# A three-layer graph network on one core: comparisons of the first layer written for two groups of edges at a time

## The chip, the cores and the metric

The kernel runs on one core of one Trainium2 chip. The metric is device time in microseconds (us) for one execution of the whole program. Before the change the median of three runs is 2081.6 us (2081.57 to 2082.88). Profiles come from one further execution with the hardware profiler on; times inside a profile count from its first instruction.

## The reference, cut to what matters

There are 6250 nodes with 256 features and 100000 edges sorted by their target. Each of three graph layers multiplies by a weight matrix and sums the rows of the neighbours, scaled by the degrees of both ends.

```python
src = concatenate([edge_index[0], loops])        # every node is also its own neighbour
dst = concatenate([edge_index[1], loops])
deg = segment_sum(ones, dst); dinv = rsqrt(deg)
norm_edge = dinv[src] * dinv[dst]
for W, b in ((W1, b1), (W2, b2), (W3, b3)):      # 256 -> 512 -> 512 -> 256
    h = relu(segment_sum((h @ W)[src] * norm_edge[:, None], dst) + b)
return layernorm(x + h)
```

## The kernel before, in words

The nodes are cut into 50 blocks of 125 (`Q`). A layer needs, for each block, the sum over all edges that end in it. There are two ways to get this sum.

**Gathered blocks.** For blocks 22 to 49 of layer 1 (`every[FEW:]`), GpSimd (POOL) issues indirect DMAs that fetch 128 source rows at a time (L1192). The VectorE (DVE) compares target numbers with the columns 0 to 124 to make a 0/1 matrix `shot` (L1143), and TensorE (PE) multiplies the two into a sum (L1219). One fetch is one *chunk* of the schedule; layer 1 has 451 chunks. Product and fetch stand 5 chunks apart, later 8 (`SPLIT`).

**Dense blocks.** For blocks 0 to 21 (`few`) the kernel builds the 125 x 6250 matrix of edge counts and multiplies it by all of x: 50 products of 125x125 by 125x512 per block (L1283), 1100 in all. The counts come as bytes; ScalarE (ACT) casts five 125-column cuts at a time into a `piece` (L1151).

**Making the counts** is the generator `counts`, which also serves seven more blocks for later layers: 29 blocks in all. Each block has 25 groups of at most 128 edges (`GB`), one group for 5 target nodes. For a group, DVE makes two 0/1 matrices by comparison (`compared`, L799): `hot_lo`, 125 columns, for the source's place in its block, and `hot_key`, 250 columns, for the source's block and the target's place among 5. One bf16 product of the two (L866) gives 125 x 250 counts in PSUM. Two groups share a PSUM bank, and ACT writes both as bytes into a *place* (L828). When all 25 are there, DVE adds the self loops (L819), the counts are stored to HBM (`kept`), and the dense products of that block may begin from the next chunk on (`there`). The comparisons are written for five groups together (`WIDE`): 625 elements of `hot_lo`, then 750 and 500 of `hot_key`. Their operands are `near_cols`, fp32 numbers in PSUM, and `slots`, bf16 numbers in SBUF, and they write bf16.

**The order of the work** is written out by hand: `layer` walks over the chunks, and in each it emits a fetch, the product of an earlier fetch, one step of each waiting generator (`go`, `go_fixed`) and up to three dense products. Each engine then works through its own list in that order. `counts` yields twice in five of its steps, so 25 groups take 10 chunks. A product for the counts is emitted four steps behind its comparison. Banks come from the list `common`; at most three counted banks may wait for ACT (`COUNTING`). Dense products are due from chunk `first` = 16 on, at 50 per 19 chunks, never more than three in a chunk.

Around the start of layer 1, `parts` (x split in a high and a low part, one slice per block) is ready for blocks 20 to 49; `other_parts` (L1485, L1487) makes blocks 15-19, then 0-4, 5-9 and 10-14 in the first chunks. The places for the counts lie on the memory from which these are made. `both_stored` stores `parts` to HBM meanwhile, and `windows` looks up the next groups of edges. At the end of layer 1, `teams` (L993 and what feeds it) begins to load its data over the upper blocks of `parts` when all but 16 dense products are emitted.

`after1` finishes a block: L1304 transposes, L1330 multiplies by the weights, L1335 and L1338 add the bias and scale.

## Time and profile before

| | us |
|---|---|
| median of three runs | 2081.6 |
| the profiled execution | 2088.76 |
| its span, first to last instruction | 2086.9 |
| PE busy in the span | 1937.8 |
| DVE busy in the span | 1350.6 |
| comparisons for the counts (L799), 75 to 700 us | 324.87 |

The profiled execution is 7.2 us above the median, of which 1.9 us lie outside its span. The mean granted TensorE clock is 0.981. Layer 1 lies at about 75 to 700 us of the span, layer 2 follows until about 1650 us, and layer 3 ends it. In the lists below, "PE" is a matmul and "PEld" the load of its stationary operand; a count such as x2 is how many instructions were merged in a row, and what stands in brackets is the idle time of the engine before the row and what ended it. A matmul's end is modelled: one that takes 270 ns in a row can be followed by the next after about 110 ns.

### The profile page before, as it was taken

The numbers are of one execution on the slowest core, as the hardware profiler recorded it, in microseconds if no ns is written. First come the engines' busy times: TensorE is split into PE (matmuls) and PEld (weight loads), VectorE is DVE, ScalarE is ACT, GpSimd is POOL, SyncE is SP. The second block draws the span as 40 slices with busy tenths as digits, with TensorE's granted clock in tenths as the row PEclk, the third lists the DMA queues.
The fourth block names the chain that finished last, engine by engine and source line by source line (L and its number), as shares of the span: only waits on it lengthen the run. The fifth ranks groups of instructions, "written<-read, shape, count | busy, mean of one in ns | idle before, by whom it ended". The sixth has DMA issues, their size and how long they took to land.

```text
span 2086.9 us, 28961 instructions
## 1 busy us (share of the span) xinstructions
PE 1937.8 (93%) x8642; PEld 1516.1 (73%) x8642; DVE 1350.6 (65%) x2385; ACT 1266.8 (61%) x2230; POOL 1406.4 (67%) x1442
## 2 busy tenths in 40 slices
PE   4499999999999788989999999999988899999997
PEld 3377777777776566778888778886766677877785
DVE  6877888887882376777677777766666234434444
ACT  2566777787784566666666666666554455555552
POOL 2467777766777377777776776676666277777775
PEclk9999999999999899999999999999999999999998
DMA  8898999999999999999999999988897599999998
GB/s 173 248 300 218 275 259 255 273 255 261 272 274 254 266 259 257 256 253 273 262 259 262 261 261 264 264 240 239 243 278 232 150 282 291 294 291 298 293 291 219
DMA packets 266157, 540.24 MB, mean 259 GB/s; under 512 B 44142, under 2 KB 77857, under 8 KB 265990
## 3 DMA queue, kind: packets, MB, share of 16 engines
q0 software_dynamic: 157728, 360.04, 63.2%
q1 hardware_dynamic: 94980, 168.96, 29.8%
q10 hardware_dynamic: 13282, 9.30, 1.7%
q8 instruction: 70, 1.15, 0.2%
q14 instruction: 97, 0.79, 0.1%
HBM read 464.28 MB, written 73.87 MB: 258 GB/s over the span
## 4 chain that ended last, share of the span: by engine, by line
PE 63%; DMA 15%; issue 7%; POOL 5%; ACT 3%; DVE 3%; SPq 0%; POOLq 0%; ACTq 0%; DVEq 0%
PE sacc L1219 12%; DMA room<-tab,ssrc 8%; PE smm L1283 7%; PE win_ps L1283 7%; PE mat_ps L1283 7%; PE sacc L1283 5%; DMA back<-tab,ssrc 4%; PE win_ps L1385 4%; POOL room L1192 4%; PE win_ps L1401 2%; PE sacc L1330 2%; PE str L1283 2%; PE sacc L993 1%; PE sacc L866 1%; PE mat_ps L993 1%
## 5 line engine op out<-in xcount | busy, mean ns | idle before, releaser
L1192 POOL DMA_INDIRECT room<-tab,ssrc x442 | 465.2, 1053 | 192.5 <-issue 81.7
L1219 PE MATMUL sacc<-halves,shot 128*125 128x512 f32 x1541 | 535.3, 409 | 25.2 <-ACT halves L1250 11.2
L1151 ACT CAST piece<-room 125x625 fp32r<-125x625 uint8 x501 | 358.0, 723 | 211.5 <-PE win_ps L1283 72.5
L1192 POOL DMA_INDIRECT halves<-both,ssrc x384 | 361.3, 941 | 142.0 <-issue 40.4
L1192 POOL DMA_INDIRECT halves<-tab,ssrc x336 | 317.2, 944 | 103.6 <-PE sacc L1219 26.5
L1219 PEld LDWEIGHTS sacc<-halves,shot 128*125 128x125 f32 x1541 | 288.3, 188 | 114.5 <-DVE halves L1253 21.6
L799 DVE TENSOR_TENSOR back<-near_cols,slots 128x625 bf16<-128x625 f32 (+2 forms) x435 | 324.9, 801 | 29.7 <-PE sacc L866 12.8
L1143 DVE TENSOR_TENSOR shot<-near_cols,sdlo 128x500 fp32r<-128x500 f32 x371 | 247.4, 668 | 134.3 <-PE sacc L1219 128.5
L1253 DVE TENSOR_TENSOR halves<-room,halves 128x512 fp32r<-128x512 f32 x334 | 227.0, 691 | 121.2 <-ACT halves L1250 114.9
L1192 POOL DMA_INDIRECT back<-tab,ssrc x230 | 231.7, 1008 | 109.1 <-issue 38.6
L1250 ACT CAST halves<-room 128x512 fp32r<-128x512 f32 x334 | 202.1, 618 | 154.2 <-DMA room<-tab,ssrc 125.4
L1385 PE MATMUL win_ps<-back,w_sb 128*128 128x250 f32 x768 | 185.3, 385 | 13.8 <-ACT back L1362 10.8
L1283 PE MATMUL smm<-parts,piece 125*125 125x512 f32 x655 | 188.7, 405 | 1.6 <-ACT piece L1151 1.6
L1283 PE MATMUL win_ps<-parts,piece 125*125 125x512 f32 x650 | 185.2, 404 | 0.0
L1385 PEld LDWEIGHTS win_ps<-back,w_sb 128*128 128x128 f32 x768 | 148.6, 195 | 39.4 <-ACT back L1362 12.9
L1283 PE MATMUL mat_ps<-parts,piece 125*125 125x512 f32 x600 | 172.0, 404 | 0.5 <-ACT piece L1151 0.5
L866 PEld LDWEIGHTS <-back 128*125 128x125 bf16 x725 | 96.0, 138 | 73.5 <-issue 22.9
L1283 PE MATMUL sacc<-parts,piece 125*125 125x512 f32 x450 | 147.7, 432 | 0.9 <-ACT piece L1151 0.9
L828 ACT CAST room<-sacc 125x500 uint8<-125x500 f32 (+1 forms) x155 | 107.5, 711 | 55.5 <-PE sacc L866 41.0
L1283 PEld LDWEIGHTS win_ps<-parts,piece 125*125 125x125 f32 x650 | 119.4, 188 | 30.0 <-issue 2.5
L1283 PEld LDWEIGHTS smm<-parts,piece 125*125 125x125 f32 x655 | 116.8, 187 | 29.4 <-issue 2.3
L1253 DVE TENSOR_TENSOR halves<-back,halves 128x512 fp32r<-128x512 f32 x136 | 93.1, 691 | 65.4 <-ACT halves L1250 64.5
(337 smaller groups left out, 3304.8 us busy)
## 6 DMA issues: line engine op xcount, KB each, us to landing
parts<-tab SPq DMA_DIRECT2D x76, 448.0 KB
kept<-room SPq DMA_DIRECT2D x29, 683.6 KB
room<-kept SPq DMA_DIRECT2D x29, 683.6 KB
both<-parts SPq DMA_DIRECT2D x10, 1120.0 KB
tab<-st SPq DMA_DIRECT2D x50, 224.0 KB
own_row<-tab SPq DMA_DIRECT2D x38, 224.0 KB
parts<-kept SPq DMA_DIRECT2D x60, 136.7 KB
room<-tab,ssrc POOLq DMA_INDIRECT x442, 6.2
```

Of the source, the lines that this page charges most:

```text
L799: nc.vector.tensor_tensor(out, near_cols[:, :shape[2]].unsqueeze(1).to_broadcast(shape), numbers.unsqueeze(2).to_broadcast(shape), op=ALU. ...
L828: nc.scalar.copy(place[:, :, u * G:(u + len(ms)) * G].rearrange("p k (t r) -> p t k r", r=G), counted_in[:Q, :len(ms) * 256].rearrange("p ...
L866: nc.tensor.matmul(bank[:Q, len(pair) * 256:][:, :G * NB], lhsT=hot_lo, rhs=hot_key, start=True, stop=True)
L993: nc.tensor.matmul(team_banks[n][:, :TEAM * Q], lhsT=both_parts[u % 3][:, h * HID + n * P:h * HID + (n + 1) * P], rhs=team_pieces[(g * CUT ...
L1143: nc.vector.tensor_tensor(hot[:, :n], near_cols[:, :Q].unsqueeze(1).to_broadcast([P, n, Q]), dlo.rearrange("p b j -> p (b j)")[:, at:at + ...
L1151: nc.scalar.copy(piece, made_or_read[:, c * PIECE:(c + 1) * PIECE, :])
L1192: nc.gpsimd.indirect_dma_start(out=row, out_offset=None, in_=table, in_offset=bass.IndirectOffsetOnAxis(ap=at, axis=0))
L1219: nc.tensor.matmul(acc[:Q, :size], lhsT=hot, rhs=row[:, c0:c0 + size], start=(i == 1 and k == c0 == 0), stop=(k == KF and c0 + size == row ...
L1250: nc.scalar.copy(halves[:, :width], landed[chunk - hi_lag])
L1253: nc.vector.tensor_sub(halves[:, width:], landed.pop(chunk - lo_lag), halves[:, :width].bitcast(F32))
L1283: nc.tensor.matmul(acc_d[:Q], lhsT=got[done // PIECE][:, k % PIECE, :], rhs=parts[:, k], start=(k == 0), stop=(k == NB - 1))
L1385: nc.tensor.matmul(h_ps[:, f, :], lhsT=w2_sb[:, k, (f2 + f) * P:(f2 + f + 1) * P], rhs=zt[:, k, :], start=(k == 0), stop=(k == KH - 1))
```

## The change

It does three things, in layer 1 alone.

1. **Comparisons.** Groups go in units of two, 12 units and one single group per block. `slots` gets a pitch of 26 for 25 groups, so that each pair begins on a 4-byte boundary. The column numbers for the comparison stand in PSUM as bf16, each number twice in a row (`near_keys`). The outputs are laid out with the two groups of a unit next to each other in each column, so that numbers, columns and output all have two 16-bit elements in their innermost dimension. `hot_lo` is compared for two units at once, 500 elements; `hot_key` per unit, 500 elements; the last group alone with 125 and 250 elements. The operands of L866 are then read with a step of two elements.
2. **Steps.** The first block's counts are emitted with three yields of their own in place of ten, later blocks with ten in 13 steps; products follow their comparison by two steps. `first` becomes 12.
3. **Order of the dense products.** Each dense block starts with row blocks 20 to 49, then takes 15-19, 10-14, 5-9 and 0-4. `other_parts` makes 0-4 first, then 5-9, 15-19, 10-14. `teams` starts to load when all but 15 products are emitted.

```diff
+TAIL = 4
-WIDE = 5
+TWO = 2
+WIDE = 2 * TWO
...
-    slots = one.enter_context(tc.tile_pool(name="sslots", bufs=1, side="right")).tile([P, NW, 2, Q], BF16, name="slots")
+    numbered = one.enter_context(tc.tile_pool(name="sslots", bufs=1, side="right"))
+    slots = numbered.tile([P, NW, 2, Q // GB, GB + 1], BF16, name="slots")
+    keys = numbered.tile([P, G * NB, 2], BF16, name="keys")
...
-            nc.vector.tensor_copy(keys, keys_i)
+            nc.vector.tensor_copy(keys, keys_i.unsqueeze(2).to_broadcast([P, G * NB, 2]))
...
-    near_cols = near[:, :G * NB]
-    nc.vector.tensor_copy(near_cols, keys)
+    near_cols = near[:, :Q]
+    nc.vector.tensor_copy(near_cols, cols[:, :Q])
+    nc.vector.tensor_copy(near[:, P:P + G * NB], keys.rearrange("p k t -> p (k t)").bitcast(F32))
+    near_keys = near[:, P:P + G * NB].bitcast(BF16).rearrange("p (k t) -> p k t", t=2)
...
         def compared(out, numbers):
-            shape = list(out.shape)
-            nc.vector.tensor_tensor(out, near_cols[:, :shape[2]].unsqueeze(1).to_broadcast(shape),
-                                    numbers.unsqueeze(2).to_broadcast(shape), op=ALU.is_equal)
+            _, pairs, wide, size = out.shape
+            nc.vector.tensor_tensor(out, near_keys[:, :wide, :size].unsqueeze(1).to_broadcast([P, pairs, wide, size]),
+                                    numbers.rearrange("p (j t) -> p j t", t=size).unsqueeze(2).to_broadcast([P, pairs, wide, size]),
+                                    op=ALU.is_equal)
...
-        total = len(blocks) * GB
+        units = [(n, u, min(TWO, GB - u)) for n in range(len(blocks)) for u in range(0, GB, TWO)]
+        total = len(units)
...
-            if s < total and s % WIDE == 0:
-                t, w = divmod(blocks[s // GB] * GB + s % GB, Q)
-                hot_stores.rotate(-1)
...
-                compared(hot_lo, slots[:, t, 0, w:w + WIDE])
-                compared(hot_key[:, :3], slots[:, t, 1, w:w + 3])
-            if s < total and s % WIDE == 2:
...
-                compared(hot[s // WIDE][1][:, 3:], slots[:, t, 1, w:w + WIDE - 3])
+                t, row = divmod(blocks[n], Q // GB)
+                at = u // TWO % 2 if size == TWO else 0
+                if size < TWO:
+                    alone = hot_stores[-1][:, WIDE * (Q + G * NB):].rearrange("p (j v t) -> p j v t", j=1, t=1)
+                    hot_lo, hot_key = alone[:, :, :Q], alone[:, :, Q:]
+                elif at == 0:
+                    hot_stores.rotate(-1)
...
+                if at == 0:
+                    width = min(WIDE, GB - u)
+                    compared(hot_lo, slots[:, t, 0, row, u:u + width])
+                compared(hot_key[:, at:at + 1, :, :size], slots[:, t, 1, row, u:u + size])
+                hot[s] = [(hot_lo[:, at, :, v], hot_key[:, at, :, v]) for v in range(size)]
             copied(ticks)
-            m = s - 4
+            m = s - TWO
...
-                nc.tensor.matmul(bank[:Q, len(pair) * 256:][:, :G * NB], lhsT=hot_lo, rhs=hot_key, start=True, stop=True)
...
-            if s % WIDE in (2, 4):
+                for v, (hot_lo_v, hot_key_v) in enumerate(hot.pop(m)):
+                    nc.tensor.matmul(bank[:Q, v * 256:][:, :G * NB], lhsT=hot_lo_v, rhs=hot_key_v, start=True, stop=True)
+                full.append((ticks + COPIED, bank, [n * GB + u + v for v in range(size)]))
+            if s % (GB // TWO + 1) % 4 != 3 and (s > GB // TWO or s % 2):
                 ticks += 1
                 yield 1
...
-        while products < FEW * NB - KF:
+        while products < FEW * NB - HOME // PIECE * PIECE:
...
+            c = order[c]
             nc.scalar.copy(piece, made_or_read[:, c * PIECE:(c + 1) * PIECE, :])
...
+        order = (*range(TAIL, CUTS), *range(TAIL - 1, -1, -1)) if i == 0 else range(CUTS)
...
-                    nc.tensor.matmul(acc_d[:Q], lhsT=got[done // PIECE][:, k % PIECE, :], rhs=parts[:, k],
+                    nc.tensor.matmul(acc_d[:Q], lhsT=got[done // PIECE][:, k % PIECE, :], rhs=parts[:, order[k // PIECE] * PIECE + k % PIECE],
                                      start=(k == 0), stop=(k == NB - 1))
...
-        for g, h in ((GRP, PIECE), (0, 0), (0, PIECE), (GRP, 0)):
+        for g, h in ((0, 0), (0, PIECE), (GRP, PIECE), (GRP, 0)):
...
-    first = 16
+    first = 12
```

More of the change, by code (lines that the diff above doesn't have):

```diff
@@ L553, in windows @@
         yield LATE
-        nc.scalar.copy(slots[:, t], sl_ps.rearrange("p (t v) -> p t v", t=2)[:, :, :Q])
+        nc.scalar.copy(slots[:, t, :, :, :GB], sl_ps.rearrange("p (t v) -> p t v", t=2)[:, :, :Q].rearrange("p t (b u) -> p t b u", u=GB))
         common.append(sl_ps)
@@ L585, in sorted_path @@
         zero = dp1.tile([1, HID], F32, name="szero")
-        keys = const.tile([P, G * NB], BF16, name="keys")
         own_i = dp1.tile([Q, 1], I32, name="sown_i")
@@ L730, in sorted_path @@
     late_place = scratch[:Q, :MW].bitcast(U8)[:, :NB * Q].rearrange("p (k v) -> p k v", v=Q)
-    HW = -(-WIDE * (Q + G * NB) // 2 // 4) * 4
-    hot_rooms = [back[:, n * HW:][:, :HW].bitcast(BF16)[:, :WIDE * (Q + G * NB)] for n in range(2)]
-    late_hot_room = back[:, 2 * HW + 2 * C:][:, :HW].bitcast(BF16)[:, :WIDE * (Q + G * NB)]
+    HW = -(-(WIDE + 1) * (Q + G * NB) // 2 // 4) * 4
+    hot_rooms = [back[:, n * HW:][:, :HW].bitcast(BF16)[:, :(WIDE + 1) * (Q + G * NB)] for n in range(2)]
+    late_hot_room = back[:, 2 * HW + 2 * C:][:, :HW].bitcast(BF16)[:, :(WIDE + 1) * (Q + G * NB)]
     first_rows = [back[:, at:at + C] for at in range(2 * HW, BACK - 4 * C - C + 1, C)]
@@ L850, in counts @@
             copied(ticks)
-            m = s - 4
+            m = s - TWO
             if 0 <= m:
-                while m % GB == 0 and not place_for(m // GB):
+                n, u, size = units[m]
+                while u == 0 and not place_for(n):
                     ticks += 1
@@ L856, in counts @@
                     copied(ticks)
-                while bank is None:
+                while True:
                     bank = bank_for_pair()
-                    if bank is None and full and full[0][0] <= ticks + COPIED - 2:
+                    if bank is not None:
+                        break
+                    if full and full[0][0] <= ticks + COPIED - 2:
                         copied(full[0][0])
-                    elif bank is None:
+                    else:
                         ticks += 1
```

23 lines of the change are left out of this document (9 added, 14 removed).

## The prediction, made before the changed kernel was built or run

> **What bounds the kernel now.** I read the page first, then the stretches of layer 1, then who waited for whom there, then the start in order of time.
>
> ```profile
> PE 1937.8 (93%) x8642; PEld 1516.1 (73%) x8642; DVE 1350.6 (65%) x2385; ACT 1266.8 (61%) x2230; POOL 1406.4 (67%) x1442
> ```
> ```profile
> core 0: us, PE busy (x) PEld busy (x) DVE busy (x) ACT busy (x) POOL busy (x), PEclk, DMA share, GB/s
> 75.00:650.00 575.00, 554.05 (x2639) 412.40 (x2640) 462.12 (x766) 419.89 (x733) 410.42 (x432) 1.00 0.93 262
> 126.00:650.00 524.00, 518.86 (x2477) 385.90 (x2476) 417.48 (x696) 391.51 (x687) 374.53 (x399) 1.00 0.94 262
> ```
>
> From 126 to 650 us PE is busy 518.86 of 524 us: 5.1 us idle. From 75 to 126 us it idles 51 - (554.05 - 518.86) = 15.8 us. DVE is busy 417.48 of 524 us (80%), much, but PE sets the pace. So whatever DVE gains can come back only out of these 21 us, and the question is who ended them.
>
> ```profile
> PE sacc L866 <- DVE back L799: 16.0, 3, 13.1
> PE mat_ps L1219 <- DMA back<-tab,ssrc: 3.1, 1, 3.1
> PE str L866 <- DVE back L799: 1.7, 1, 1.7
> PE sacc L1219 <- DMA back<-tab,ssrc: 1.6, 2, 1.4
> PE sacc L1219 <- DMA room<-tab,ssrc: 1.4, 1, 1.4
> PE smm L1283 <- ACT piece L1151: 0.7, 1, 0.7
> PE smm L866 <- DVE back L799: 0.7, 1, 0.7
> PE sacc L866 <- DVE w_sb L520: 0.3, 1, 0.3
> ```
> ```profile
> 78.45 1.30 PE L866 MATMUL sacc<-back 128*125 128x250 bf16 x5 [13.13 <-DVE back L799]
> 82.00 0.37 PE L866 MATMUL sacc<-back 128*125 128x250 bf16 x1 [2.24 <-DVE back L799]
> 86.52 1.19 PE L1219 MATMUL mat_ps<-back,shot 128*125 128x256 f32 x2 [3.10 <-DMA back<-tab,ssrc]
> 91.02 1.06 PE L1219 MATMUL mat_ps<-back,shot 128*125 128x256 f32 x2
> 93.30 0.59 PE L1219 MATMUL mat_ps<-back,shot 128*125 128x256 f32 x2
> 98.86 3.79 DVE L799 TENSOR_TENSOR back<-near_cols,slots 128x625 bf16<-128x625 f32 x5
> 100.55 0.27 PE L866 MATMUL str<-back 128*125 128x250 bf16 x1 [1.68 <-DVE back L799]
> 102.56 0.34 DVE L819 TENSOR_TENSOR room<-room,loops 125x125 uint8<-125x125 uint8 x1
> 102.99 1.95 ACT L1151 CAST piece<-room 125x625 fp32r<-125x625 uint8 x3 [1.43 <-DVE room L819]
> 103.75 0.96 PE L1283 MATMUL smm<-parts,piece 125*125 125x512 f32 x3 [0.73 <-ACT piece L1151]
> ```
>
> The first list is the waits of 75 to 126 us (total, times, longest), the second the timeline. The 13.1 us end at 78.45 with the first comparison, and 2.24 us more end at 82.00; neither can be won, because the first fetched rows arrive only at 86.52 and PE, in order, stands there. After 86.52 PE is short of work until the first dense product at 103.75: the waits for DVE (16.0 - 13.1 - 2.2 + 1.7 + 0.7 + 0.3 = 3.4) and for ACT (0.7), 4.1 us. The chain is one of order: the self loops of block 0 (L819) stand on DVE behind 3.79 us of comparisons that belong to block 1. The three DMA waits (3.0 us, after 118 us) are for fetches.
>
> ```profile
> PE sacc L866 <- DVE back L799: 1.3, 2, 0.7
> PE mat_ps L866 <- DVE back L799: 1.0, 1, 1.0
> PE sacc L1283 <- ACT piece L1151: 0.9, 1, 0.9
> PE str L1283 <- ACT piece L1151: 0.9, 1, 0.9
> PE mat_ps L1283 <- ACT piece L1151: 0.5, 1, 0.5
> PE smm L866 <- DVE back L799: 0.3, 1, 0.3
> ```
>
> From 126 to 660 us, DVE ended 2.6 us and ACT's casts 2.3 us of PE's idle time, and that is nearly all.
>
> **The change part by part.** The comparisons first.
>
> ```profile
> L799 DVE TENSOR_TENSOR back<-near_cols,slots 128x750 bf16<-128x750 f32 x145 | 134.8, 929 | 0.0
> L799 DVE TENSOR_TENSOR back<-near_cols,slots 128x625 bf16<-128x625 f32 x145 | 116.6, 804 | 29.7 <-PE sacc L866 12.8 <-PE str L866 5.6 <-PE mat_ps L866 4.5
> L799 DVE TENSOR_TENSOR back<-near_cols,slots 128x500 bf16<-128x500 f32 x145 | 97.2, 670 | 0.0
> ```
> ```profile
> 73.86 0.28 DVE L724 CAST keys<-keys_i 128x250 bf16<-128x250 int32 x1
> 74.24 0.42 DVE L775 CAST near_cols<-keys 128x250 f32<-128x250 bf16 x1
> ```
>
> 250 elements more cost 929 - 670 = 259 ns: 1.04 ns an element and 150 ns fixed. Five of each form per block make 5 x 2.40 = 12.0 us, and 29 blocks 349 us. After, a block has 18 comparisons of 500 elements and two of 125 and 250. No row shows a comparison at two elements at a time; the copies do show that DVE has such a rate (250 elements in 0.28 us, against 0.42 us when it writes fp32 to PSUM). Bounds: 670 ns each if nothing gains, 150 + 260 = 410 ns at the double rate. I take 410, since all three operands become 16-bit with pairs side by side. Then a block costs 18 x 0.41 + 0.28 + 0.41 = 8.1 us, 29 blocks 234 us: DVE loses 115 us of work. Nearly all of that is beside PE and worth nothing by itself.
>
> [...]
>
> *Set-up:* one more copy of 125 elements (0.28 us) and twice the elements in the copy at 73.86 (+0.13 us). The first fetch waits for this copy, so its rows arrive **0.4 us** later, and with them PE's 86.52.
>
> *First block:* before, 23 comparisons (18.5 us) stand on DVE ahead of L819. Counting the loop, at most three banks wait for ACT, so the first block still takes some 13 chunks instead of 15, but only eight comparisons of block 1 are emitted before L819: 8.1 + 8 x 0.41 = 11.4 us, 7 us less. PE then has to do what it did between 86.5 and 103.75 minus its stalls, so the dense products start at about 97 to 98 us, and the 4.1 us go. Each of the six waits also hides some 0.16 us of the matmul's modelled length (a lone product lasts 0.27 us, a following one adds 0.11). **-5 us**; bounds 0 and -7. What is late next are the fetches, for which PE already waits 3.0 us while the stores of `both` run beside them; they come no sooner than POOL and the DMA rings bring them. I add **+1 us** of DMA waits; bounds 0 and +3, twice the waits of now.
>
> *Clock:* the same pair of products takes 1.06 us at 91.02 and 0.59 us at 93.30: until some moment between them PE runs at about half speed. [...]
>
> *Steady part:* the 2.6 us for DVE, with the hidden part, **-3 us** (bounds 0 and -4); ACT's work is unchanged and its 2.3 us stay.
>
> ```profile
> 426.02 1.52 PE L1283 MATMUL sacc<-parts,piece 125*125 125x512 f32 x3
> 429.00 0.95 PE L1283 MATMUL sacc<-parts,piece 125*125 125x512 f32 x3
> ```
>
> The waits of 1.0 us for DVE and 0.9 us for ACT come together just before the first of these rows, and three products then take 1.52 in place of 0.95 us, the second row. Some three microseconds go by so; I take **-1 us** for this, bounds 0 and -1.5.
>
> *The products L866* stay 725 in number; only the step of their operands changes.
>
> ```profile
> 126.88 0.38 PE L866 MATMUL sacc<-back 128*125 128x250 bf16 x2
> 127.12 0.94 PE L1283 MATMUL smm<-parts,piece 125*125 125x512 f32 x3
> 128.47 0.70 PE L1283 MATMUL smm<-parts,piece 125*125 125x512 f32 x2
> ```
>
> Two of L866 last 0.38 us and one (at 100.55) 0.27: one more adds 0.11 us for 250 columns of two bytes (0.44 ns a column). One more of L1283 adds 0.24 us for 512 columns of four bytes (0.47 ns). Columns four bytes apart are thus read at the same rate, and I cost the new step at **0**; bounds 0 and twice the time, 725 x 0.11 = 80 us.
>
> *Order of dense products:* each product reads other blocks, none costs more; `other_parts` issues the same eight instructions in another order, early in the layer. Cost 0. *`first` = 12* brings dense work four chunks forward, 4 x 2.63 x 0.235 = 2.5 us of PE ahead of the same fetch.
>
> ```profile
> 640.03 0.94 POOL L1192 DMA_INDIRECT halves<-both,ssrc  x1 [0.30 <-PE sacc L1219]
> 684.65 0.94 POOL L1192 DMA_INDIRECT halves<-both,ssrc  x1 [2.83 <-PE win_ps L1219]
> ```
>
> From 640 us on the fetches follow each other every 0.94 + 0.30 = 1.24 us, as fast as POOL issues them, and the last one at 684.65 ends the layer. What PE does earlier there makes these fetches later by up to 2.5 us; `teams` starts earlier in return, so I put **+2 us**, bounds -2 and +3.
>
> **Sum:** 0.4 - 5 + 1 - 1 - 3 - 1 + 2 = -6.6 us. The profiled execution would go from 2088.8 to 2082.2 us. It lies 7.2 us above the median of the runs, none of it in layer 1's steps, so the median goes from 2081.6 to **2075.0 us**. Layers 2 and 3 shift as they are.
>
> **The rivals.**
>
> *TensorE reads the pairs more slowly* (slower). If a step of two elements halves its rate, L866 costs 80 us more on the engine that sets the end: 2155 us. It decides from 6.6 / 725 = 9 ns a product, and from 15 ns the kernel is slower beyond what can be told. Against it: the four-byte columns of L1283 above. For it: no bf16 operand in the trace is read with a gap. Chance 0.08.
>
> *The comparisons stay at one element a cycle.* Then a block costs 18 x 0.67 + 0.69 = 12.8 us, DVE gets 21 us more in layer 1 and is 84% busy; ahead of L819 stand 12.8 + 8 x 0.67 = 18.1 us, as before, so the start gains nothing, and the steady waits for DVE stay or grow by 1 or 2 us. About 2083 us. Chance 0.09.
>
> *The fetches take the gain.* POOL can issue 451 x 1.24 = 560 us of fetches in the 611 us from the copy that it waits for (74.24 + 0.42) to 685.6, and since 640 us it has no room. If the start's DMA waits grow by as much as DVE frees and the tail stays at POOL's pace, 1 or 2 us are left: 2080 us. For it: a DMA share of 0.93. Against it: 50 us of slack over the layer. Chance 0.12.
>
> *All of PE's idle time goes*, ACT's part too, because DVE also ends the steps between products earlier: -15 us, 2066 us. Chance 0.05.
>
> **How the numbers follow.** The forecast has 0.66, from 2069 to 2080 us by the bounds of its terms. About 0.2% (4.2 us) is what a measurement of this kernel can tell from no change. The forecast lies under 2077.4 us in seven of eight cases: 0.57, and with the last rival 0.62 for faster. Same: 0.09 of the forecast, 0.12, and 0.06 of the comparisons' rival: 0.27. Slower: 0.08 and 0.03: 0.11. The range from 2064 to 2086 us holds all but the rival of TensorE and the edges of the others.
>
> **What would show it.** Right: the rows of L799 become 18 of 500 elements per block at about 410 ns, with both operands 16-bit; DVE's comparisons fall from 325 to about 230 us; one more L866 still adds 0.11 us; the first dense product comes at 97 to 98 us; PE's waits for L799 after 86 us go, and those for ACT stay; the last fetch of layer 1 is issued at about 678 us, and the later layers have the same length. Wrong: 670 ns comparisons (second rival); L866 pairs above 0.38 us or PE still full with a longer layer 1 (first); new waits of L1219 for DMA between 95 and 130 us, or a last fetch at 683 us or later (third).

## The result and the profile after

The changed kernel takes 2101.4 us (median of 4 runs, 2098.0 to 2102.7); the kernel before took 2081.6 us beside it (4 runs). The ratio is 1.0091, with a 95% interval of 1.0072 to 1.0111. The change makes the kernel 19.8 us slower; 2075.0 us were forecast, and the time lies outside the range of 2064 to 2086 us. In the lists of the changed kernel the lines have moved: L804 are the comparisons (L799 before), L881 the products for the counts (L866), L1297 the dense products (L1283), L1206 and L1233 the fetches and their products (L1192, L1219).

Each comparison took the time that was forecast. The groups of DVE between 75 and 700 us, kept apart by form:

```profile
L804 DVE TENSOR_TENSOR back<-near_cols,slots 128x500 bf16<-128x500 bf16 x522 | 189.8, 410 | 111.4 <-PE sacc L881 51.9 <-PE smm L881 23.1 <-PE win_ps L881 14.0
L804 DVE TENSOR_TENSOR back<-near_cols,slots 128x250 bf16<-128x250 bf16 x29 | 11.9, 410 | 0.0
L804 DVE TENSOR_TENSOR back<-near_cols,slots 128x125 bf16<-128x125 bf16 x29 | 8.2, 282 | 0.0
```

That is 18 comparisons of 500 elements a block at 410 ns; those of 125 and 250 elements, with a single element in their innermost dimension, gain nothing though all their operands have 16 bits: 282 and 410 ns, against 285 and 414 ns with fp32 numbers in PSUM (a_single_rate, below). Added up, the 580 comparisons are the forecast 234 us. DVE is busy with them for only 204.3 us (324.9 before), since comparisons that follow each other overlap: six in a row take 2.04 us, not 6 x 0.41 = 2.46. Of the list of stretches, the two that were shown of before, and of the waits of TensorE the lists for 75 to 126 us (four rows) and 126 to 660 us (four rows):

```profile
75.00:650.00 575.00, 557.65 (x2653) 418.70 (x2654) 344.07 (x911) 423.78 (x738) 402.43 (x426) 1.00 0.93 261
126.00:650.00 524.00, 520.91 (x2483) 390.05 (x2482) 310.94 (x825) 393.81 (x689) 370.50 (x394) 1.00 0.94 261
```
```profile
PE sacc L881 <- DVE back L804: 13.2, 2, 12.3
PE sacc L1233 <- DMA back<-tab,ssrc: 5.5, 1, 5.5
PE mat_ps L1233 <- DMA back<-tab,ssrc: 3.6, 2, 2.1
PE sacc L1218 <- ACT room L835: 1.5, 1, 1.5
...
PE smm L1233 <- DMA halves<-both,ssrc: 1.2, 2, 1.1
PE smm L1233 <- DMA back<-tab,ssrc: 0.9, 1, 0.9
PE mat_ps L1233 <- DMA back<-tab,ssrc: 0.6, 1, 0.6
PE sacc L881 <- DVE back L804: 0.3, 1, 0.3
```

From 126 to 650 us DVE has 107 us less to do, and TensorE idles 3.1 us in place of 5.1. Up to 660 us, 0.3 us of its waits for DVE are left, and ScalarE's casts (2.3 us before) are gone from the list too. At the start, the waits for fetched rows took the place of those for DVE. The timeline shows the first dense product, and a pair of counting products at the length they had (0.39 and 0.27 us):

```profile
88.38 1.19 PE L1233 MATMUL sacc<-back,shot 128*125 128x256 f32 x2 [5.48 <-DMA back<-tab,ssrc]
99.39 0.96 PE L1297 MATMUL win_ps<-parts,piece 125*125 125x512 f32 x3
127.19 0.39 PE L881 MATMUL str<-back 128*125 128x250 bf16 x2
128.57 0.27 PE L881 MATMUL sacc<-back 128*125 128x250 bf16 x1
```

So by 100 us the kernel is 4.4 us ahead. The loss comes later. These are GpSimd's last fetch of layer 1 and first of layer 2 in the changed kernel, then the first of layer 2 in the kernel before (its last of layer 1 stood at 684.65):

```profile
695.99 1.13 POOL L1206 DMA_INDIRECT halves<-both,ssrc  x1 [0.30 <-issue]
...
716.69 0.96 POOL L1206 DMA_INDIRECT room<-tab,rest  x1 [19.58 <-DMA tab<-st]
```
```profile
709.13 0.96 POOL L1192 DMA_INDIRECT room<-tab,rest  x1 [23.54 <-DMA parts<-tab]
```

I cut each profile at the first fetch of a layer. Layer 1 lasts 642.9 us against 634.4 (+8.5), layer 2 948.6 against 941.5 (+7.1), layer 3 435.6 against 436.2. With a start 1.0 us earlier these make the 14.0 us by which the spans differ. The other 5.9 us to the medians are the profiled execution of before, 7.2 us above its median, less the 1.3 us of this one. Layer 2, which the change doesn't touch, is thus half of the question.

**Layer 1's end.** SyncE's queue around the end, of the changed kernel and of the kernel before (start, length, merged rows of DMA issues; `tab<-st` stores finished blocks, `parts<-kept` and `parts<-tab` load for the teams):

```profile
642.06 3.26 SPq L81 DMA_DIRECT2D parts<-kept  x8
653.82 3.35 SPq L81 DMA_DIRECT2D parts<-tab  x6
657.22 10.44 SPq L81 DMA_DIRECT2D parts<-kept  x8
667.75 8.58 SPq L79 DMA_DIRECT2D tab<-st  x6
```
```profile
636.00 27.98 SPq L77 DMA_DIRECT2D tab<-st  x10
664.09 4.36 SPq L79 DMA_DIRECT2D parts<-kept  x8
668.56 4.00 SPq L79 DMA_DIRECT2D parts<-tab  x6
672.66 11.97 SPq L79 DMA_DIRECT2D parts<-kept  x8
```

Before, ten stores stand ahead of the teams' loads. After, the dense products are emitted earlier, so the 22 loads come earlier, and six of the stores stand behind them. The loads wait for the memory that TensorE still reads (two of SyncE's waits, 630 to 720 us):

```profile
SPq L81 <- PE win_ps L1218: 7.9, 1, 7.9
SPq L81 <- PE sacc L1297: 4.4, 3, 3.2
```

What follows is one chain across four engines, in the timeline of the changed kernel:

```profile
674.03 0.69 DVE L1349 TENSOR_TENSOR st<-mat_ps,back 125x512 f32<-125x512 f32 x1 [13.12 <-DMA tab<-st]
674.64 0.47 DVE L1329 SCALAR_TENSOR_TENSOR szs<-sacc,sdinv,szs 125x256 f32<-125x256 f32 x1
675.17 0.68 PE L1318 MATMUL sacc<-ident_r,szs 125*128 125x125 f32 x2 [7.71 <-DVE szs L1329]
675.51 1.20 PE L1233 MATMUL win_ps<-halves,shot 128*125 128x512 f32 x2
676.55 0.97 POOL L1206 DMA_INDIRECT halves<-both,ssrc  x1 [4.77 <-PE win_ps L1233]
```

DVE waits 13.1 us for a store before it may write the next block's `st`; behind it stands the step for which TensorE idles 7.7 us; behind that the product that frees the row for the next fetch, and GpSimd loses 4.8 us of the stream that ends the layer. The list of groups from 620 us to the end of layer 1 gives the stream's idle time, of the changed kernel, of the kernel before and of the changed kernel with `first` = 18 (below):

```profile
L1206 POOL DMA_INDIRECT halves<-both,ssrc x54 | 51.4, 951 | 26.2 <-PE win_ps L1233 11.4 <-issue 5.9 <-DMA halves<-both,ssrc 2.8
```
```profile
L1192 POOL DMA_INDIRECT halves<-both,ssrc x48 | 45.6, 949 | 20.6 <-issue 6.2 <-PE win_ps L1219 3.4 <-PE str L1283 3.2
```
```profile
L1206 POOL DMA_INDIRECT halves<-both,ssrc x50 | 46.9, 938 | 17.5 <-issue 4.0 <-PE sacc L1233 3.0 <-DMA halves<-both,ssrc 2.9
```

**Layer 2.** The two largest waits of TensorE, in the changed kernel and then in the kernel before:

```profile
PE sacc L1233 <- ACT halves L1264: 18.2, 9, 8.6
PE sacc L1233 <- ACT back L1376: 14.5, 6, 3.8
```
```profile
PE sacc L1219 <- ACT halves L1250: 11.2, 12, 4.4
PE win_ps L1385 <- ACT back L1362: 10.8, 6, 3.1
```

The second row of after is new. L1376 (L1362 before) is the copy in `after2` that empties a sum bank; the kernel before never has a gathered product waiting for it. One such place in the timeline:

```profile
976.24 0.82 ACT L1406 ACTIVATE back<-win_ps,b_sb 128x250 f32<-128x250 f32 x2
976.95 0.57 ACT L1376 COPY back<-sacc 128x500 f32<-128x500 f32 x1
977.58 1.22 PE L1233 MATMUL sacc<-halves,shot 128*125 128x512 f32 x2 [3.77 <-ACT back L1376]
```

Layer 2 has two sum banks. Where a block begins and neither is free, the loop that writes out the order pushes earlier blocks' last steps forward one at a time until one is (`need`, `late += 1`). Then the emptying copy stands directly ahead of the product that needs the bank, and TensorE waits until ACT has come to it. Followed through the loop, the kernel before has no such **forced step** in layer 2, the changed one 12, at five blocks. (The expectations below count every forced step three times: their 12, 36, 48, 66 and 78 stand for 4, 12, 16, 22 and 26 in the program.) Whether a block finds a bank depends on where the teams stand, whose groups end in the same steps; and they begin behind 453 fetched products in place of 464.

### The profile page after: what moved, and what is told of

It is laid out like the page before. It is cut to its first block, busy times and chain, and to the rows that moved or that the text cites. A ratio compares the mean times of both kernels' runs of the same rounds, so it can differ in the third digit from the quotient of the medians.

```text
span 2100.9 us, 29145 instructions
## 1 busy us (share of the span) xinstructions
PE 1939.2 (92%) x8642; PEld 1526.6 (73%) x8642; DVE 1232.2 (59%) x2531; ACT 1266.5 (60%) x2230; POOL 1398.4 (67%) x1442
## 5 line engine op out<-in xcount | busy, mean ns | idle before, releaser
L1206 POOL DMA_INDIRECT room<-tab,ssrc x442 | 453.2, 1025 | 210.6 <-DVE halves L1267 90.8
L1233 PE MATMUL sacc<-halves,shot 128*125 128x512 f32 x1534 | 529.6, 412 | 44.1 <-ACT halves L1264 18.2
L1164 ACT CAST piece<-room 125x625 fp32r<-125x625 uint8 x491 | 350.7, 721 | 216.0 <-PE win_ps L1297 68.8
L1206 POOL DMA_INDIRECT halves<-both,ssrc x384 | 361.3, 941 | 148.9 <-issue 34.9
L1206 POOL DMA_INDIRECT halves<-tab,ssrc x336 | 317.5, 945 | 102.5 <-issue 34.5
L1233 PEld LDWEIGHTS sacc<-halves,shot 128*125 128x125 f32 x1534 | 291.9, 192 | 127.8 <-ACT halves L1264 22.7
L1206 POOL DMA_INDIRECT back<-tab,ssrc x230 | 235.3, 1023 | 119.0 <-DVE halves L1267 35.8
L1267 DVE TENSOR_TENSOR halves<-room,halves 128x512 fp32r<-128x512 f32 x337 | 228.3, 691 | 118.2 <-ACT halves L1264 113.2
L1264 ACT CAST halves<-room 128x512 fp32r<-128x512 f32 x337 | 201.6, 618 | 128.4 <-DMA room<-tab,ssrc 117.1
L804 DVE TENSOR_TENSOR back<-near_cols,slots 128x500 bf16<-128x500 bf16 x580 | 204.3, 404 | 111.4 <-PE sacc L881 51.9
L1297 PE MATMUL win_ps<-parts,piece 125*125 125x512 f32 x750 | 219.4, 409 | 0.1
L1297 PE MATMUL mat_ps<-parts,piece 125*125 125x512 f32 x700 | 205.7, 409 | 0.0
L1297 PE MATMUL sacc<-parts,piece 125*125 125x512 f32 x500 | 166.6, 434 | 0.0
L1297 PEld LDWEIGHTS win_ps<-parts,piece 125*125 125x125 f32 x750 | 135.8, 189 | 31.7 <-issue 3.2
L881 PEld LDWEIGHTS <-back 128*125 128x125 bf16 x725 | 97.2, 140 | 70.8 <-issue 24.3
L1297 PEld LDWEIGHTS mat_ps<-parts,piece 125*125 125x125 f32 x700 | 124.4, 187 | 26.6 <-issue 2.2
L962 DVE TENSOR_TENSOR parts<-parts 125x512 fp32r<-125x512 f32 x150 | 103.3, 689 | 42.5 <-ACT parts L960 42.4
L1267 DVE TENSOR_TENSOR halves<-back,halves 128x512 fp32r<-128x512 f32 x137 | 93.7, 691 | 53.6 <-ACT halves L1264 53.3
```

Of the source, the lines that this page charges most:

```text
L804: nc.vector.tensor_tensor(out, near_keys[:, :wide, :size].unsqueeze(1).to_broadcast([P, pairs, wide, size]), numbers.rearrange("p (j t) -> ...
L881: nc.tensor.matmul(bank[:Q, v * 256:][:, :G * NB], lhsT=hot_lo_v, rhs=hot_key_v, start=True, stop=True)
L962: nc.vector.tensor_sub(to[:, HID:], row, to[:, :HID].bitcast(F32))
L1164: nc.scalar.copy(piece, made_or_read[:, c * PIECE:(c + 1) * PIECE, :])
L1206: nc.gpsimd.indirect_dma_start(out=row, out_offset=None, in_=table, in_offset=bass.IndirectOffsetOnAxis(ap=at, axis=0))
L1233: nc.tensor.matmul(acc[:Q, :size], lhsT=hot, rhs=row[:, c0:c0 + size], start=(i == 1 and k == c0 == 0), stop=(k == KF and c0 + size == row ...
```

## The experiments

Three theories stood at the beginning: A, that the early dense and team work (`first` = 12) itself holds the fetches up; B, that the start's collisions of fetches and stores do it; C, that the comparisons at double rate disturb something. After the second group of runs a fourth took A's place for layer 2: P, the forced steps. The table has every kernel in the order of its forced steps; the waits and lengths are those of one profile each, the ratio is to the kernel before in the same session.

| kernel | teams behind | forced steps | L1233 waits for L1376 | layer 2, us | DVE waits for a store | layer 1, us | ratio |
|---|---|---|---|---|---|---|---|
| before | 464 | 0 | 0 | 941.5 | 0 | 634.4 | 1 |
| b_order | 464 | 0 | 0 | 935.7 | 0 | 630.4 | 0.9992 |
| a18_single_again | 464 | 0 | 0.4 | 934.5 | 0 | 628.6 | 0.9982 |
| a_first18 | 464 | 0 | 0 | 928.0 | 0 | 632.1 | 1.0004 |
| a_first20 | 464 | 0 | 0 | 932.2 | 0 | 633.7 | 0.9995 |
| a_first26 | 468 | 0 | 2.2 | 940.0 | 3.5 | 629.6 | 0.9991 |
| a_first16 | 464 | 0 | 0 | 930.6 | 16.6 | 637.4 | 1.0013 |
| a_first13 | 464 | 0 | 0.2 | 935.8 | 20.4 | 639.3 | 1.0012 |
| a_hold12_again | 460 | 0 | 0.3 | 935.5 | 14.1 | 637.4 | 1.0037 |
| b_first12_hold10 | 461 | 0 | 0.6 | 940.3 | 17.8 | 645.7 | 1.0088 |
| a_hold4_again | 452 | 4 | 12.3 | 940.0 | 13.0 | 638.3 | 1.0034 |
| after | 453 | 12 | 14.5 | 948.6 | 13.1 | 642.9 | 1.0091 |
| a_single_rate | 453 | 12 | 14.7 | 946.6 | 13.7 | 643.1 | 1.0114 |
| b_first12 | 455 | 16 | 19.5 | 951.4 | 0 | 649.2 | 1.0174 |
| a_first24 | 476 | 22 | 7.2 | 968.7 | 0 | 630.6 | 1.0170 |
| a_hold10_again | 459 | 26 | 7.0 | 951.8 | 14.3 | 636.1 | 1.0068 |

TensorE idles 50 to 62 us of layer 2 in the ten kernels without forced steps, and 65 to 80 us in the six with them.

**`first` alone, and the comparisons alone.** a_first16 and a_first24 change one line of the changed kernel:

```diff
-    first = 12
+    first = 16        # a_first24: 24
```

> The changed kernel with first = 16 in place of 12; all else stays. Counted from the order of emission, 464 of the fetched products then stand ahead of the first product of teams on TensorE, as in the kernel before (453 in the changed one), and each dense block begins within 10 fetched products of where it did before. Theory A (dense products and teams were moved ahead of the fetch stream, and the fetch stream ends layer 1 and layer 2): at least two thirds of the 20 us come back, 2075 to 2088 us, and the last fetch of layer 1 is issued within 3 us of the kernel before (684.7). Theory B (the start: stores and first fetches collide in the DMA rings because the first block is counted sooner): nothing of that changes in the first 15 chunks, so 2094 us or more. Theory C (the fast comparisons themselves disturb another engine): 2094 us or more.

Measured: 1.0013 [1.0000, 1.0027]. Undoing one number of the change takes nearly all of the loss away, although the start of the layer stays that of the changed kernel: B falls, and C with it. The last fetch of layer 1 was issued at 688.2 us, 3.5 us after that of the kernel before, where A allowed 3.

> The changed kernel with first = 24: dense blocks begin 8 to 12 fetched products later than in the changed kernel all along, and the first product of teams stands behind all 476 fetched products. Theory A: fetches come earlier still, the last one before 680 us, and what is lost is the overlap of teams with the end of layer 1; 2070 to 2088 us. Theories B and C: 2094 us or more.

Measured: 1.0170 [1.0149, 1.0191]. Layer 1 is short (630.6 us) and layer 2 the longest of all (968.7 us). Theory A in its simple form, the later the better, fell here.

a_single_rate puts the column numbers back to fp32 in PSUM, so that the comparisons run at the old rate again:

```diff
-    nc.vector.tensor_copy(near[:, P:P + G * NB], keys.rearrange("p k t -> p (k t)").bitcast(F32))
-    near_keys = near[:, P:P + G * NB].bitcast(BF16).rearrange("p (k t) -> p k t", t=2)
+    near_keys = near[:, P:P + G * NB]
+    nc.vector.tensor_copy(near_keys, keys[:, :, 0])
...
-            nc.vector.tensor_tensor(out, near_keys[:, :wide, :size].unsqueeze(1).to_broadcast([P, pairs, wide, size]),
+            nc.vector.tensor_tensor(out, near_keys[:, :wide].unsqueeze(1).unsqueeze(3).to_broadcast([P, pairs, wide, size]),
```

> The changed kernel with the column numbers of the comparison as fp32 in PSUM, each read for both groups; outputs, order and steps stay. The 500-element comparisons should take about 670 ns in place of 404. Theory C: the loss goes, 2090 us or less. Theory A: the order of emission is that of the changed kernel, so it stays at 2096 to 2108 us; it may be some us slower since VectorE is busier. Theory B: as A, or some us faster since the start is slower.

Measured: 1.0114 [1.0091, 1.0136], against 1.0091 of the changed kernel. The rate neither causes the loss nor relieves it, and C is out here too. The row of its comparisons:

```profile
L804 DVE TENSOR_TENSOR back<-near_cols,slots 128x500 bf16<-128x500 f32 x522 | 322.5, 672 | 32.7 <-PE sacc L881 22.4 <-PE str L881 3.9 <-PE smm L881 3.6
```

b_order gives the kernel before the third part of the change alone (`order`, the order of `other_parts`, and the teams' start at 15):

```diff
+            c = order[c]
...
+        order = (*range(TAIL, CUTS), *range(TAIL - 1, -1, -1)) if i == 0 else range(CUTS)
...
-        while products < FEW * NB - KF:
+        while products < FEW * NB - HOME // PIECE * PIECE:
...
-        for g, h in ((GRP, PIECE), (0, 0), (0, PIECE), (GRP, 0)):
+        for g, h in ((0, 0), (0, PIECE), (GRP, PIECE), (GRP, 0)):
```

> The kernel before with the third part of the change alone: dense products from row block 20 on, other_parts in the new order, teams released at all but 15 products. The order of emission of fetched products, dense blocks and teams is that of the kernel before. Theory A: no difference, 2078 to 2086 us. Theory B in the form that other_parts' new order holds up the start: 2087 us or more.

Measured: 0.9992 [0.9976, 1.0008]. This part is worth nothing and costs nothing.

**Dense lead against teams' lead.** With `first` = 13 the dense products stand as early as with 12, but the teams as before. With 18 and 20 both are about as before. b_first12 is the kernel before with `first = 12` in place of 16.

> The changed kernel with first = 13 in place of 12. Counted in TensorE's list, dense blocks still stand about as early among the fetched products as with 12 (the last one behind 430 of them, 429 with 12, 437 before), but the first team product stands behind 464 fetched products as before the change, not behind 453. Theory (the early dense and team work is what costs; the two leads cost about 9 us each): about 2092 us, 1.004 to 1.006 of the kernel before; last fetch of layer 1 still at 693 to 697 us, the stretch from the first fetch of layer 2 to that of layer 3 back at 930 to 942 us. If the lead of the dense products alone carries the loss: as the changed kernel, 1.008 to 1.010. If the lead of the teams alone carries it: as with first = 16, 1.000 to 1.003.

Measured: 1.0012 [0.9997, 1.0028]. The forecast was missed; what was measured is what was named for the case that the teams' lead alone carries the loss. In the profile layer 1 keeps a part of its loss (its last fetch stands at 689.1 us, earlier than expected), and layer 2 has none. One step of `first` is worth 0.8%, with the dense products where they were.

> The kernel before with first = 12 and nothing else. First team product behind 455 fetched products, dense blocks behind 12, 29, ..., 433. Theory (order of work alone): slower by 8 to 18 us, 1.004 to 1.009, with no change to the comparisons at all. Rival (the new comparisons or their steps are what costs, and first only brings it out): within 0.2% of the kernel before.

Measured: 1.0174 [1.0153, 1.0194], nearly twice the forecast. The loss needs neither the new comparisons nor the new steps. Layer 1 is the longest of all here (649.2 us), with no wait for a store. Its timeline shows another wait of the same origin:

```profile
677.71 0.62 ACT L948 CAST parts<-parts 125x512 fp32r<-125x512 f32 x1 [6.89 <-DMA parts<-tab]
681.09 2.07 PE L1330 MATMUL sacc<-w,back 128*125 128x512 f32 x2 [8.81 <-ACT back L1324]
684.69 0.94 POOL L1192 DMA_INDIRECT halves<-both,ssrc  x1 [7.12 <-PE sacc L1219]
```

ScalarE waits 6.9 us for a load of the teams; behind the teams' casts stands the copy (L1324) of a finished block, for which TensorE idles 8.8 us, and behind that the fetch stream loses 7.1 us.

> The changed kernel with first = 18: dense blocks behind 13, 34, 54, ..., 435 fetched products, teams behind 464 as before. Theory: a little faster than with first = 16 (1.0013 of the kernel before), 0.998 to 1.001, since the dense lead is smaller still and the teams start no later. Rival (the freed time of the comparisons is really lost somewhere in layer 1): as with 16 or more, 1.001 to 1.003.

Measured: 1.0004 [0.9987, 1.0021].

> The changed kernel with first = 20: dense blocks behind 15, 36, 56, ..., 437 fetched products, the last as before the change, teams behind 464 as before. Theory: the dense products start later, so PE is short of work in the first 20 chunks by up to 4 x 0.6 us, and the tail is as before or shorter: 0.998 to 1.001. If the late dense work was the whole cause of the loss with 24 (1.017): about 1.004 to 1.008; if it was the late start of the teams there (behind 476 in place of 464): as with 18.

Measured: 0.9995 [0.9981, 1.0009]. With 464 fetched products ahead of the teams, nothing is lost that can be told; with 453, 455 and 476 about 1% and more. That isn't a matter of early or late. Followed through the loop, the first group has no forced steps in layer 2, the second 12, 16 and 22.

**The teams' pause.** These change the teams' start alone, in the changed kernel:

```diff
         fetch_counts(0, 2)
-        yield 6
+        yield 4           # a_hold10: 10, a_hold12: 12
```

> The changed kernel with the teams' own pause after their first loads shortened from 6 to 4 steps (yield 6 in teams becomes yield 4). The teams then begin behind 452 fetched products in place of 453: even a little earlier. Two theories of the loss in layer 2. Theory P (forced steps): layer 2 has two sum banks, and where a new block needs one that is not yet free, the loop that writes the order pushes the earlier blocks' ends forward until it is (need, late); then the ACT copy that frees the bank stands directly ahead of the product that needs it, and TensorE waits for ACT to get there. Counted in the order, the changed kernel has 36 such forced steps in layer 2 (at five blocks), this one 12 (at one block), the kernels of ratio 1.000 to 1.001 have none, the two of 1.017 have 48 and 66. By P: 1.003 to 1.007, and TensorE's waits of L1233 for the copy of L1376 fall from 14.5 us to about 5. Theory A (the earlier the teams, the worse): as the changed kernel or worse, 1.009 to 1.011.

> The changed kernel with the pause of the teams at 10 steps: they begin behind 459 fetched products, between the changed kernel (453) and the kernel before (464). Forced steps in layer 2: 78, at three blocks. Theory P (forced steps): slower than the changed kernel, 1.015 to 1.022. Theory A (the earlier the teams, the worse): between the two, about 1.004.

> The changed kernel with the pause of the teams at 12 steps: they begin behind 460 fetched products, one later than with a pause of 10; dense products, comparisons and all of layer 1 to the end of the dense products as in the changed kernel. Forced steps in layer 2: none. Theory P: 0.999 to 1.002, no waits of L1233 for L1376. Theory A: about 1.003 to 1.004, as with a pause of 10.

> The changed kernel with first = 18, which has no forced steps in layer 2 (ratio 1.0004 to the kernel before), but with the numbers of hot_key's columns in fp32 in PSUM, so that the comparisons run at one element a cycle again (about 670 ns for 500 elements, 371 us in all in place of 234). This is what the double rate is worth with the order of the work out of the way. As the prediction priced it (about 4 to 9 us of TensorE's waits that go): slower than with first = 18 by 0.2 to 0.4%, 1.002 to 1.005. If TensorE has enough other work in layer 1 to cover the comparisons at either rate: 0.999 to 1.002.

Measured: 1.0053 [1.0023, 1.0083], 1.0150 [1.0109, 1.0190], 1.0055 [1.0028, 1.0081] and 1.0022 [0.9997, 1.0046]. These four ran in a session in which the kernel before took 2280.6 us, and in which engines idled with nothing to wait for that the trace shows (last section); they were run again in a session like those before. Even so, hold10 and hold12, one fetched product apart, differ by 0.95% in P's sense.

> The pause of 4 steps once more, on another chip: in the session before, every engine also waited for its own instructions (idle time put down to issue), the kernel before took 2281 us there, and the ratios of all kernels came out about 0.3 to 0.5% above what was expected. Forced steps in layer 2: 12. Theory P (forced steps): 1.003 to 1.007. Theory A (the earlier the teams, the worse): 1.009 to 1.011 or more.

Measured: 1.0034 [1.0014, 1.0055], as P has it: teams even earlier than in the changed kernel, and less lost. A falls for layer 2. The waits of L1233 for L1376 missed P's forecast, though: 12.3 us in place of about 5.

> The pause of 10 steps once more. Forced steps in layer 2: 78. Theory P: 1.015 to 1.022. Theory A: about 1.004.

> The pause of 12 steps once more; one fetched product later than with 10, everything in layer 1 up to there the same as in the changed kernel. Forced steps in layer 2: none. Theory P: 0.999 to 1.002. Theory A: 1.003 to 1.004.

Measured: 1.0068 [1.0041, 1.0095] and 1.0037 [1.0019, 1.0055]. The sign is P's, and the profiles agree on the place: layer 2 lasts 951.8 and 935.5 us, and TensorE's waits for the copy go (of each, one row of the waits in layer 2):

```profile
PE sacc L1233 <- ACT back L1376: 7.0, 4, 2.8
```
```profile
PE sacc L1233 <- ACT back L1376: 0.3, 1, 0.3
```

The sizes aren't P's: 26 steps cost less than 12 did in the changed kernel, and none still leaves 0.37%, which is what A had forecast for it. The count tells where layer 2 loses, not how much; the rest of hold12 lies in layer 1 (637.4 us, 14.1 us of DVE's wait for a store).

a18_single is the changed kernel with `first` = 18 and the edit of a_single_rate.

> The changed kernel with first = 18 and the comparisons at one element a cycle (fp32 column numbers), once more. As the prediction priced the freed waits: 1.002 to 1.005. If TensorE has enough other work in layer 1 to cover the comparisons at either rate: 0.999 to 1.002.

Measured: 0.9982 [0.9966, 0.9997]; a_first18 had 1.0004. Both forecasts lie above it, the second just so: in an undisturbed order the double rate is worth nothing that can be told. TensorE's stretch from 126 to 620 us, in the kernel before, in a_first18 and in a18_single_again (us, TensorE busy, weight loads, DVE, ACT, GpSimd):

```profile
126.00:620.00 494.00, 488.86 (x2350) 363.78 (x2349) 409.74 (x683) 374.00 (x658) 353.18 (x376) 1.00 0.95 263
```
```profile
126.00:620.00 494.00, 493.36 (x2375) 371.10 (x2374) 303.64 (x812) 378.50 (x667) 351.39 (x373) 1.00 0.95 263
```
```profile
126.00:620.00 494.00, 493.60 (x2374) 370.70 (x2373) 415.48 (x810) 378.27 (x666) 352.92 (x374) 1.00 0.96 264
```

The 5.1 us that TensorE idled shrink to 0.6 and 0.4 us at either rate, in a18_single_again with DVE busier than before (415 us): so it isn't the rate that removed them. Nor is it the order of the dense products, with which alone b_order idles 6.0 us. The steps (products two steps behind their comparisons) remain as the likely cause; no run separates them from `first` = 18.

**Taking the forced steps away from the two slowest.** a_first26 (`first = 26`) beside a_first24, and b_first12_hold10 (`first = 12` and `yield 10` in the kernel before) beside b_first12:

> The changed kernel with first = 26: dense blocks later still than with first = 24 (behind 22, 42, ..., 444 fetched products), teams behind 468. Forced steps in layer 2: none, against 66 with first = 24 (ratio 1.017, layer 2 969 us from first fetch to first fetch of layer 3). Theory P (forced steps carry the loss of layer 2): layer 2 back at 928 to 941 us and the ratio at 0.998 to 1.004. If it was the late dense and team work that cost with 24: 1.010 or more.

> The kernel before with first = 12 (ratio 1.0174, 48 forced steps in layer 2, layer 1 649 and layer 2 951 us) and the pause of the teams at 10 steps in place of 6, so that they begin behind 461 fetched products and there is no forced step. Theory P with the early work's own share in layer 1: layer 2 back at 928 to 941 us, layer 1 shorter than 649 by what the teams no longer put ahead of its last fetches, ratio 1.003 to 1.010. If the forced steps carry nothing: 1.012 or more.

Measured: 0.9991 [0.9972, 1.0010] in place of 1.0170, with dense products later still, and 1.0088 [1.0065, 1.0110] in place of 1.0174. Layer 2 falls from 968.7 to 940.0 us and from 951.4 to 940.3 us. Layer 2 of a_first24, then of a_first26:

```profile
703.00:1672.00 969.00, 889.44 (x3900) 722.17 (x3898) 644.09 (x1023) 592.19 (x1090) 632.11 (x613) 0.97 0.88 248
```
```profile
703.00:1644.00 941.00, 886.93 (x3867) 714.79 (x3866) 642.39 (x1018) 587.86 (x1082) 638.28 (x613) 0.97 0.89 253
```

TensorE is busy 889 and 887 us in the two; it idles 80 us in the one and 54 in the other. Of these 26 us the waits of L1233 for L1376 are only 5.0. A larger part is another wait in the same blocks' last steps, that of the transposes (L1318) for VectorE's step ahead of them (L1361), here in a_first24 and then in a_first26:

```profile
PE sacc L1318 <- DVE szs L1361: 15.1, 5, 10.6
```
```profile
PE sacc L1318 <- DVE szs L1361: 4.0, 5, 1.6
```

a_hold10_again has 11.6 us of it and a_hold12_again 2.0; all the others have at most 7.1 us.

No version beats the kernel before by what can be told: the best, a18_single, has 0.9982 in one session and 1.0022 in the other.

## Why the prediction was wrong

**The comparisons** came out as forecast: 410 ns each. (DVE's busy time with them fell to 204, not to about 230 us, because they overlap.) 16-bit operands alone are not enough for this rate by the runs: with one element innermost, 250 elements still took 410 ns. For 500 elements in pairs the two rows are 672 ns with fp32 column numbers in PSUM (a_single_rate) and 410 ns with 16-bit ones there. What the prediction and two expectations call one element a cycle is the rate of the rows before, 1.04 ns an element. **L866** with its new step costs nothing, as forecast (0.39 - 0.27 = 0.12 us for one more product). The first dense product came at 99.4, not 97 to 98 us, and the first fetched rows 1.9 us later than before (88.4 us), not 0.4.

**The gains** were given back at once or lay elsewhere. At the start, -5 us became 4.4 us of lead for the dense products, but the layer isn't ended by dense products; DMA waits rose by 3.0 us from 6.1 to 9.1 us, the bound of the term, where +1 was taken. No run shows the -1 us put down for the clock. What the two profiles show is that a pair of fetched products (L1233) lasts 0.59 us from 92.49 us on (1.02 us at 91.40), before (L1219) from 93.30 us on, with a granted clock from 75 to 126 us of 0.97, and of 1.00 before; what these 0.8 us are worth in the time of the whole was not separated. The -3 and -1 us of the steady part are real as idle time of TensorE (5.1 us to 0.6 us with `first` = 18, ACT's part with them, which the prediction let stand), but not by the faster comparisons, and no run shows them in the time of the whole: with `first` at 18 and 20 the ratio is 1.0004 and 0.9995.

**The step that failed is "`first` = 12", put down as +2 us with bounds of -2 and +3.** The two profiles show +8.5 us in layer 1 and +7.1 us in layer 2, and 1.0091 against 1.0012 when `first` alone goes to 13 or 1.0013 at 16. b_first12 shows that this step alone makes the kernel before slower (1.0174). The prediction counted the teams' earlier start as a gain and left out two mechanisms.

- In layer 1 it asked only what TensorE does ahead of the same fetch. The teams' 22 loads, which it moved, were not followed past SyncE's queue, where they now stand ahead of the stores of finished blocks. Seven kernels have 0 to 3.5 us of DVE's wait and a layer 1 of 629 to 634 us (`first` = 16 in the kernel before, 18 and more in the changed one); the eight with 13 to 20 us of this wait have 636 to 646 us. The exception is b_first12, at 649 us without it: there the teams' load holds up ScalarE in place of the stores. Both chains are read from the traces; no run took the loads out of the way alone, so for layer 1 the cause is argued and not shown by an experiment. The prediction also took the fetches from 640 us on to run at GpSimd's own pace (1.24 us a fetch); the last row that it shows, at 684.65 us, itself waits 2.83 us for a product of TensorE.
- In layer 2 it said "layers 2 and 3 shift as they are". They don't shift: the teams run from layer 1 into layer 2, and their lead sets which blocks find a sum bank. Ten kernels without forced steps have a layer 2 of 928 to 942 us, six with them 940 to 969 us, and L1233 waits 0 to 2.2 us and 7.0 to 19.5 us for L1376. Three pairs bear out that the forced steps are the cause (hold10 and 12, `first` 24 and 26, b_first12 with a pause of 6 and 10): in each, the kernel without forced steps has the shorter layer 2, by 16, 29 and 11 us, although its teams start later in two of the pairs and earlier in one. Each pair moves the teams as well, if only by 1 to 8 products; no run takes the forced steps out of an order that stays as it is otherwise (a third sum bank would). How large the loss is for a given count stays open: a forced step also runs other blocks' last steps early (the wait of L1318 above), and those were not separated.

**The rivals.** "The fetches take the gain" named the right stream, but as the end of a gain, at 2080 us; it is where a loss begins. The comparisons at the old rate would have cost nothing that can be told. "All of PE's idle time goes" came nearly true from 126 to 620 us in a_first18, and brought nothing. The range came from terms of layer 1 alone; without the 80 us set aside for the first rival, their bounds (0 and -2 us for the clock) add up to 2065.5 and 2088.0 us, not to the 2069 and 2080 us that are named, and neither could hold the result.

## What to carry to other kernels

When a step moves, follow each DMA that it issues past the queue it lands in: here loads that waited 7.9 and 4.4 us for memory stood ahead of six stores, and by the trace the price was paid in steps that have nothing to do with the loads (13.1 us of VectorE's wait, 7.7 of TensorE's, 4.8 of GpSimd's). An order written out by a program reacts to its inputs in jumps: count its corrective steps (here: a bank that had to be forced free) before and after, in every stage, since one step in the start of a background stream was worth 0.3 to 0.8% and the faster instruction nothing. Where one engine is 99% busy, as TensorE here (518.86 of 524 us), put a faster neighbour down as worth its waits at most (2.6 us here, of which the time of the whole showed nothing); see first whether a change of order alone removes them.

## What the runs showed of the hardware that was not expected

In one session the kernel before took 2280.6 us (29 runs) and in the others 2080 to 2083 us. The record gives the number 3 to the chip of that session, and the same number to the chip of the last two runs, where it took 2082.1 us; so whether it was the chip is not shown. The instructions nearly kept their durations: in a_hold12 there and in the changed kernel, which differs from it by the teams' pause alone, 410 and 410 ns for a comparison of 500 elements, 412 and 412 ns for L1233 (`sacc<-halves,shot`). But engines stood idle with nothing to wait for that the trace shows, put down to issue: in a_hold12 97 us of TensorE in all, 39.2 us of VectorE ahead of one group (L1267) and 34.9 us of ScalarE ahead of another (L1264); in the changed kernel 0, 8.5 and 10.4 us of the three engines in all. One group of TensorE in a_hold12:

```profile
L1297 PE MATMUL win_ps<-parts,piece 125*125 125x512 f32 x750 | 226.4, 413 | 13.5 <-issue 11.6 <-ACT piece L1164 0.8 <-ACT room L835 0.4
```

In the changed kernel the same group lasts 409 ns a product and idles 0.1 us. What the engines waited for there isn't known. A ratio to the kernel before in the same session corrects only a part of it: hold10 had 1.0150 there and 1.0068 later.
